# A graph kernel with neighbour sorts: lists found in words of two scores, sorts that leave two columns out, and single-graph sets

## The chip, the cores and the metric

The kernel runs on one core of a Trainium2 chip. The core has five engines with a queue each: TensorE (PE), VectorE (DVE), ScalarE (ACT), GpSimd (POOL) and SyncE (SP). Each works through its instructions in the order in which the program put them, and waits where an operand is not ready. SP issues plain DMAs, POOL the indirect ones. The metric is the device time of one execution in microseconds, the median of several runs; lower is better.

## The reference, cut to what matters

There are 16 graphs of 1024 nodes with 64 features each, and an adjacency matrix for every graph. Layer 0 is a dense message step and a small network. Layer 1 takes, for every node and every feature, three quantiles over the node's neighbours, after a rule has removed up to two of them.

```python
# layer 0
messages = einsum('bij,bjh->bih', adjacency, h)
dh = tanh(concatenate([h, messages], -1) @ W1 + b1) @ W2 + b2
x = layernorm(x + dh)
# layer 1
adj_d = dilate(adj, mask)          # degree m > 10: skip = (m+1)//2, drop every skip-th neighbour
vals = where(valid[..., None], x[:, None, :, :], big)
sv = sort(vals, axis=2)
for tau, wt in zip([0.25, 0.5, 0.75], [0.25, 0.5, 0.25]):
    pos = tau * (m - 1)            # linear interpolation between sv[floor] and sv[ceil]
    agg += wt * q
x = layernorm(x + mlp(x + agg) * mask)
```

The adjacency is sparse and its degree falls with the node number: a few nodes have more than a hundred neighbours, most have under ten.

## The kernel before, in words

The kernel gathers neighbours instead of masking. Its work is written as some twenty generators ("jobs"), which `run_jobs` (L323) interleaves.

**Scheduler.** `Engine` (L234) wraps each engine: it estimates a cost for every instruction and keeps on a `Board` when each engine comes free and when each tile is written. `run_jobs` always takes the step of the job with the smallest `max(ready, engine free) + bias`. A job that moves to another engine gets `HOP` (L214, 1000 ns) added to its ready time. Biases stand in the list at the end of `sparse`: `front` is -300 ns on DVE and -1500 elsewhere, sorts have 0, the ends of units -2000. The resulting order is fixed when the program is built; on the chip each engine follows it.

**Front, per graph.** SP loads adjacency tiles (`a_sb`). DVE makes `score`, a float16 for each neighbour that falls with the column and is 0 elsewhere; SP stores the scores to `score_rows`. PE transposes the tiles and multiplies them into messages, and `layer0` (L617) adds the network and the norm: `pre` and `s_rows` on DVE. The rows go to `score_rows`, to `table`, and for the sets of two graphs to a table of their own, `early`. `places` (L658) ranks nodes by degree.

**Sets.** `SETS` (L194) groups graphs: two pairs and three fours. Within a set, tile `q` takes 128 nodes of like degree, `128 // len(graphs)` from each graph; tile 0 holds the hubs. `LIMITS` bounds the neighbours of a node by its rank. POOL fetches a tile's scores and rows with one indirect DMA (`permuted`, 128x578 words). `listing` (L766) finds the neighbours of its nodes: rounds of `max` (the 8 largest of a row) and `match_replace` (set those to 0). `remove` scatters the removed edges into the tables, so a set's first tiles ("heads") have to be listed before anything is gathered.

**Hubs.** `CLASSES` (L204) collects hub rows of several graphs into tiles of 128: `first_tile` (L856) stores their scores, `hub_lists` (L1064) lists them. The two greatest classes, 1 and 0, are `pair` and the great hub unit; their buffers exist only when the front's memory is free.

**Units.** `UNITS` (L206) groups one to four tiles into a unit, and `plan` orders units and hubs. Per unit:
- `fetch_rows` (L1098) issues one indirect gather on POOL for each neighbour slot of each tile: `X[:, d, k, :]`, 128 rows of 66 words. The last two columns carry what the removals overwrite. `XBUFS` is 4.
- `prepare` compares those two columns with the node's number (`hit`), and ACT adds a very large value (`fill`) to removed neighbours.
- `sort` (L971) runs a merge-exchange network over the slots with `min` and `max` between `X` and `Y`, on DVE.
- `finish` scales the sorted slots with interpolation weights on ACT and sums them on PE (`pa`), runs the network, and POOL scatters the result into `out_dram`.

Nearly all instructions carry the line of the recording helper, so the profile is read by tile names.

Of the kernel before, what the change touches and what calls it, by code (L numbers as in the profile page):

```python
# [11 lines left out]
F32 = mybir.dt.float32  # L12
F16 = mybir.dt.float16
# [10 lines left out]
P = 128  # L24
N = 1024
NT = N // P
C = 64
# [145 lines left out]
def network(n, inner):  # L173
# [5 lines left out]
    for layer in needed_only(merge_exchange(n), need):  # L179
        new = {}  # L180
        for cost, at, ops in beam:
# [9 lines left out]

SETS = ((0, 1), (2, 3), (4, 5, 6, 7), (8, 9, 10, 11), (12, 13, 14, 15))  # L194
ROWS = N + 1
W = C + 2
NX = N // 2 + W
# [3 lines left out]
          (192, 11), (256, 10), (288, 9), (352, 8), (448, 7), (544, 6), (672, 5), (800, 4),  # L201
          (896, 3), (992, 2))

CLASSES = ((0, 8, 16), (8, 8, 16), (16, 8, 16), (24, 8, 16), (32, 32, 4))  # L204

UNITS = {2: ((1,), (2, 3), (4, 5, 6, 7), (8, 9, 10, 11), (12, 13, 14, 15)),  # L206
         4: ((1,), (2,), (3, 4), (5, 6, 7)) + tuple(tuple(range(q, q + 4)) for q in range(8, 32, 4))}
HEADS = 256
PIECE = 1056
# [1 line left out]
AHEAD = 6  # L211
LISTS = 2
XBUFS = 4
HOP = 1000  # L214
LANDS = 1500


def most(slot):

    return min(cap for first, cap in LIMITS if first <= slot)  # L220
# [137 lines left out]
def sparse(ctx, tc, x, adj, nodemask, w1a, b1a, w2a, b2a, w1b, b1b, w2b, b2b, consts, out,  # L358
# [3 lines left out]
    B = x.shape[0]  # L362
    set_of = {b: i for i, graphs in enumerate(SETS) for b in graphs}
    board = Board()
    V, A, T, GP, SY = (Engine(e, k, board) for e, k in zip(
        (nc.vector, nc.scalar, nc.tensor, nc.gpsimd, nc.sync), "VATGS"))
# [5 lines left out]
    fpool = fronts.enter_context(tc.tile_pool(name="s_front", bufs=1))  # L372
# [64 lines left out]
    with tc.tile_pool(name="s_init", bufs=1) as pool:  # L437
# [16 lines left out]
        for b in range(B):  # L454
            V.tensor_copy(info[:, b, :, 0], node_id)
            V.memset(info[:, b, :, 4], float(b - SETS[set_of[b]][0]))
            V.tensor_copy(counts[:, b, NT:], rev)
# [4 lines left out]
    none = fpool.tile([B, W], F32, name="s_none")  # L462
# [4 lines left out]
    for b in range(4, B):  # L467
# [1 line left out]
    tables = dram_disjoint_views(table, B // 4)  # L469

    early = [dram.tile([len(graphs) * ROWS, W], F32, name=f"early{graphs[0]}")
             for graphs in SETS if len(graphs) == 2]
    for t in early:
        SY.dma_start(t.rearrange("(b n) w -> b n w", n=ROWS)[:, N, :], none[0:2, :])
    hub_scores = [dram.tile([B * n, NX], F32, name=f"hub_scores{c}")
                  for c, (_, n, _) in enumerate(CLASSES)]
    hub_infos = [dram.tile([B * n, HI], F32, name=f"hub_infos{c}")
                 for c, (_, n, _) in enumerate(CLASSES)]
    score_rows = [dram.tile([len(graphs) * N, NX], F32, name=f"score_rows{graphs[0]}")
                  for graphs in SETS]  # L480
    own_rows = [dram.tile([len(graphs) * N, W], F32, name=f"own_rows{graphs[0]}")
                for graphs in SETS]
    writes = len(CLASSES) + sum(len(u) for graphs in SETS for u in UNITS[len(graphs)])
    outs = iter(dram_disjoint_views(out, writes))
# [31 lines left out]
    tiles, inputs, turned, scores, nodes, whole = {}, {}, {}, {}, {}, {}  # L516
# [240 lines left out]
    def list_fetches(pool):  # L757
        for n, (i, q) in enumerate(later):
# [4 lines left out]
            permuted(pool, si, q, "permuted", LISTS)  # L763
            yield "G", 0

    def listing(pool, si, qs, kind):  # L766

        K, state = len(qs), sets[si]
        w = P // len(SETS[si])
        caps = [most(q * w) for q in qs]  # L770
        rounds = -(-caps[0] // 8)
        lists = pool.tile([P, K, rounds * 8], F16, tag=f"lists_{kind}", name="lists", bufs=2)
        if -(-caps[-1] // 8) < rounds:
            V.memset(lists[:, :, 8:], 0.0)
        for k, q in enumerate(qs):
            yield "S", lambda q=q: (si, q) in whole
            ps = whole[si, q]
            yield "S", ps
            SY.dma_start(own_rows[si][q * P:(q + 1) * P, :], ps[:, N // 2:])
            yield "V", ps  # L780
            scores = ps[:, :N // 2].bitcast(F16)
            for r in range(-(-caps[k] // 8)):
                if r:
                    V.match_replace(scores, lists[:, k, r * 8 - 8:r * 8], scores, 0.0)
                V.max(lists[:, k, r * 8:r * 8 + 8], scores)
            done[kind] += 1
        sl = slice(qs[0], qs[-1] + 1)
        inf = state["inf"]
        return lists, dict(
            ids=inf[:, sl, 0], degree=inf[:, sl, 2], mask=inf[:, sl, 1],  # L790
            own_rows=[own_rows[si][q * P:(q + 1) * P, :] for q in qs], caps=caps,
            own=state["own"][:, sl] if kind == "headed" else None,
            out_index=[state["out_ids"][:, q:q + 1] for q in qs])
# [12 lines left out]
    def late_lists(pool):  # L806
        for i, (si, c, qs) in enumerate(plan):
            if c is None and qs[0] * P // len(SETS[si]) >= HEADS:
                yield "S", lambda si=si: done["heads"] > si
                lists, u = yield from listing(pool, si, qs, "listed")  # L810
                u["index"] = indices(pool, si, qs, lists)
                units[i] = u
# [158 lines left out]
    def sort(u):  # L971

        X = u["X"]
        _, D, K, _ = X.shape
        inner = K * W
        bufs = u["bufs"] = [X, u["Y"]]

        def wires(i, a0, n1, s1, n2, s2):
            t = bufs[i]
            dims = [t.ap[0]]  # L980
            if n1 > 1:
                dims.append([s1 * inner, n1])
            if n2 > 1:
                dims.append([s2 * inner, n2])
            return bass.AP(tensor=t.tensor, offset=t.offset + a0 * inner,
                           ap=dims + [[1, inner]])

        for kind, sa, sb, d, so, (a0, n1, s1, n2, s2) in network(D, inner)[0]:
            to = 0 if kind == "min" else d
            many = max(1, PIECE // (n2 * inner))  # L990
            for i in range(0, n1, many):
                a, n = a0 + i * s1, min(many, n1 - i)
                V.tensor_tensor(wires(so, a + to, n, s1, n2, s2), wires(sa, a, n, s1, n2, s2),
                                wires(sb, a + d, n, s1, n2, s2),
                                op=ALU.min if kind == "min" else ALU.max)
                yield "V", 0
# [137 lines left out]
    plan = []  # L1134
    for si, graphs in enumerate(SETS):
        for qs in UNITS[len(graphs)]:
            plan.append((si, None, qs))
            if si == len(SETS) - 1 and qs[-1] == 4:
                plan += [(si, 3, (0,)), (si, 2, (0,))]
        if si == 1:  # L1140
            plan.append((si, 4, (0,)))
    hubs = [i for i, p in enumerate(plan) if p[1] is not None]
    heads = [(si, q) for si, graphs in enumerate(SETS) for q in range(1, HEADS * len(graphs) // P)]
    later = [(i, q) for i, (si, c, qs) in enumerate(plan) for q in qs
# [13 lines left out]
    def fetches(pool):  # L1158
        for i, (si, c, what) in enumerate(plan):
            yield "G", lambda i=i, si=si: i in units and done["heads"] > si  # L1160
            if i >= XBUFS:
                yield "G", lambda i=i: done["free"] > i - XBUFS
            u = units[i]
            u["X"] = pool.tile([P, u["caps"][0] + 1, len(what), W], F32, tag="X", name="X",
                               bufs=XBUFS)
            src = table
            if c is None:
                src = early[si] if si < len(early) else tables[SETS[si][0] // 4]
            elif c == 4:
                src = tables[0]  # L1170
            yield from fetch_rows(u, src)
            done["fetch"] += 1
# [66 lines left out]
    with tc.manual_schedule(engines={getattr(mybir.EngineType, e) for e in  # L1239
                                     ("DVE", "Activation", "PE", "Pool", "SP")}):  # L1240
        pool = ctx.enter_context(tc.tile_pool(name="s_body", bufs=2, side="right"))

        def all_fronts_out():
            yield from front_outs(fpool)
            yield "V", lambda: done["rows"] == B
            fronts.close()
            late["pool"] = ctx.enter_context(tc.tile_pool(name="s_hubs", bufs=1))

        def front(engine):
            return -300 if engine == "V" else -1500  # L1250

        def great_bias(engine):
            return 1000 if late.get("sorting") == 0 else -500

        run_jobs(board, [
            Job(ends(pool), -2000),
            Job(preparations(pool), -1000),
            Job(loads(fpool), 0),
            Job(score_tiles(fpool), front),
            Job(sign_tiles(fpool), front),  # L1260
            Job(store_tiles(), front),
            Job(places(fpool), front),
            Job(turn_tiles(fpool), front),
            Job(head_fetches(fpool), front),
            Job(list_fetches(pool), -300),
            Job(late_lists(pool), -300),
            Job(message_tiles(fpool), front),
            Job(layer0(fpool), front),
            Job(all_fronts_out(), front),
            Job(hub_units(pool), -500),  # L1270
            Job(fetches(pool), 0),
            Job(sorts(pool), 0),
            Job(great_fetches(), -700),
            Job(great_units(), great_bias),
        ])
# [512 lines left out]
```

## Time and profile before

| | |
|---|---|
| timed, median of 3 | 3262.88 us (3250.48 to 3291.58) |
| profiled execution | 2980.74 us |
| its span, first to last instruction | 2979.0 us |
| ACT busy, instructions | 1275.4 us, 3836 |
| mean granted PE clock | 0.619 |
| HBM read and written | 159.25 MB, 56.43 MB |
| first and last store of layer-0 rows | 131.8 and 1164.9 us |
| first `permuted` fetch on POOL | 191.7 us |
| first gather of `pair` | 1326.3 us |

The profiled execution and the timed runs differ by 282 us. The views give durations within the profiled one.

The groups of instructions that weigh most (engine, operation, tiles, count, then busy us and mean ns, then idle time before them and what ended it):

```profile
L308 POOL DMA_INDIRECT X<-table,index x756 | 869.9, 1151 | 245.4 <-issue 218.2
L308 POOL DMA_INDIRECT X<-table,hub_ix x256 | 312.4, 1220 | 79.4 <-issue 74.4
L308 DVE TENSOR_TENSOR Y<-X 128x528 f32<-128x528 f32 (+11 forms) x440 | 270.8, 637 | 7.0 <-PE pa L308 3.7
L308 DVE SCALAR_TENSOR_TENSOR score<-a_sb,s_desc 128x1024 f16<-128x1024 f32 x128 | 155.1, 1219 | 104.3 <-DMA a_sb<-in_adj_dram 60.6
```

"issue" is time in which the engine waited for nothing that the profile shows.

### The profile page before, as it was taken

The numbers are of one execution on the slowest core, as the hardware profiler recorded it, in microseconds if no ns is written. First come the engines' busy times: TensorE is split into PE (matmuls) and PEld (weight loads), VectorE is DVE, ScalarE is ACT, GpSimd is POOL, SyncE is SP. The second block draws the span as 40 slices with busy tenths as digits, with TensorE's granted clock in tenths as the row PEclk, the third lists the DMA queues.
The fourth block names the chain that finished last, engine by engine and source line by source line (L and its number), as shares of the span: only waits on it lengthen the run. The fifth ranks groups of instructions, "written<-read, shape, count | busy, mean of one in ns | idle before, by whom it ended". The sixth has DMA issues, their size and how long they took to land.

```text
span 2979.0 us, 23139 instructions
## 1 busy us (share of the span) xinstructions
PE 1264.5 (42%) x5017; PEld 792.8 (27%) x5017; DVE 2148.9 (72%) x4918; ACT 1275.4 (43%) x3836; POOL 1883.6 (63%) x1609
## 2 busy tenths in 40 slices
PE   3767675758566773110413023222234131133337
PEld 2444343434343442110212001221112121111116
DVE  3337678867788876999991058878888887876782
ACT  3666575657666753120511353133243132224423
POOL 0003675265647665667687778778877778888762
PEclk9788776768767775555655555555555555555555
DMA  9555765245525532211101121221111221111100
GB/s 197 139 144 147 189 186 133 81 120 154 133 83 151 144 76 62 51 41 27 24 14 27 27 50 42 45 52 33 24 26 32 49 58 39 39 25 23 25 4 4
DMA packets 202175, 217.37 MB, mean 73 GB/s; under 512 B 136636, under 2 KB 136828, under 8 KB 202028
## 3 DMA queue, kind: packets, MB, share of 16 engines
q1 hardware_dynamic: 132140, 126.23, 15.3%
q0 software_dynamic: 57408, 86.35, 13.2%
q10 hardware_dynamic: 12480, 3.24, 1.0%
q8 instruction: 42, 0.69, 0.1%
q14 instruction: 105, 0.86, 0.1%
HBM read 159.25 MB, written 56.43 MB: 72 GB/s over the span
## 4 chain that ended last, share of the span: by engine, by line
POOL 28%; DVE 15%; issue 9%; DMA 6%; PE 3%; ACT 1%; SPq 0%; POOLq 0%; DVEq 0%; ACTq 0%
POOL X L308 24%; DVE Y L308 3%; DVE X L308 3%; DMA X<-table,index 3%; POOL out_dram L308 3%; PE pa L308 2%; DVE hub_list L308 2%; DVE hub_sc L308 1%; DVE lists L308 1%; DMA permuted<-score_rows,ids 1%; DVE pair L308 1%; POOL permuted L308 1%; DVE permuted L308 1%; DMA X<-table,hub_ix 0%; DVE pre L308 0%
## 5 line engine op out<-in xcount | busy, mean ns | idle before, releaser
L308 POOL DMA_INDIRECT X<-table,index x756 | 869.9, 1151 | 245.4 <-issue 218.2
L308 ACT ACTIVATE X<-X,fill 128x64 f32<-128x64 f32 x1248 | 315.3, 335 | 579.7 <-DVE fill L308 555.1
L308 PE MATMUL pa<-X,s_half_ident 128*128 128x64 f32 (+3 forms) x614 | 204.5, 490 | 480.0 <-ACT X L308 417.9
L308 PE MATMUL pa<-Y,s_half_ident 128*128 128x64 f32 (+3 forms) x568 | 185.3, 467 | 515.7 <-ACT Y L308 483.6
L308 POOL DMA_INDIRECT X<-table,hub_ix x256 | 312.4, 1220 | 79.4 <-issue 74.4
L308 POOL DMA_INDIRECT permuted<-score_rows,ids x128 | 138.4, 1081 | 336.3 <-DMA score_rows<-s_rows 201.0
L308 POOL DMA_INDIRECT X<-early,index x236 | 252.1, 1068 | 129.9 <-issue 68.0
L308 PEld LDWEIGHTS pa<-X,s_half_ident 128*128 128x128 f32 x614 | 141.7, 314 | 538.0 <-ACT X L308 535.5
L308 PE MATMUL pn<-aT,x_sb 128*64 128x256 f32 x1024 | 280.3, 423 | 0.0
L308 PEld LDWEIGHTS pa<-Y,s_half_ident 128*128 128x128 f32 x568 | 127.1, 296 | 572.3 <-ACT Y L308 564.3
L308 POOL DMA_INDIRECT out_dram<-y,out_ids x123 | 200.6, 1631 | 119.9 <-DVE y L308 73.3
L308 DVE TENSOR_TENSOR Y<-X 128x528 f32<-128x528 f32 (+11 forms) x440 | 270.8, 637 | 7.0 <-PE pa L308 3.7
L308 DVE MAX8 lists<-permuted 128x8 f16<-128x1024 f16 x174 | 211.2, 1222 | 35.9 <-DMA permuted<-score_rows,ids 33.6
L308 DVE SCALAR_TENSOR_TENSOR score<-a_sb,s_desc 128x1024 f16<-128x1024 f32 x128 | 155.1, 1219 | 104.3 <-DMA a_sb<-in_adj_dram 60.6
L308 DVE TENSOR_TENSOR X<-Y 128x528 f32<-128x528 f32 (+12 forms) x362 | 226.7, 642 | 2.4
L308 ACT ACTIVATE Y<-Y,wt 128x64 f32<-128x64 f32 x572 | 152.3, 335 | 150.6 <-DVE Y L308 150.6
L308 ACT ACTIVATE X<-X,wt 128x64 f32<-128x64 f32 x610 | 159.4, 334 | 131.6 <-DVE X L308 131.6
L308 PE MATMUL pt<-s_ident,a_sb 128*128 128x128 f32 x1024 | 159.3, 306 | 97.5 <-ACT aT L308 85.1
L308 ACT ACTIVATE junk<-score 128x1024 bf16<-128x1024 f16 x128 | 135.1, 1055 | 113.4 <-DVE score L308 108.6
L308 PEld LDWEIGHTS pn<-aT,x_sb 128*64 128x64 f32 x1024 | 143.9, 151 | 102.0 <-issue 49.8
L308 ACT COPY aT<-pt 128x512 f32<-128x512 f32 x256 | 137.8, 584 | 71.5 <-PE pt L308 71.1
L308 PEld LDWEIGHTS pt<-s_ident,a_sb 128*128 128x128 f32 x1024 | 128.5, 157 | 140.3 <-ACT aT L308 97.5
(168 smaller groups left out, 2804.1 us busy)
## 6 DMA issues: line engine op xcount, KB each, us to landing
a_sb<-in_adj_dram SPq DMA_DIRECT2D x128, 512.0 KB
score_rows<-score SPq DMA_DIRECT2D x128, 256.0 KB
X<-table,index POOLq DMA_INDIRECT x756
score_rows<-s_rows SPq DMA_DIRECT2D x16, 264.0 KB
table<-s_rows SPq DMA_DIRECT2D x16, 264.0 KB
x_sb<-in_x_dram SPq DMA_DIRECT2D x16, 256.0 KB
X<-table,hub_ix POOLq DMA_INDIRECT x256
own_rows<-permuted SPq DMA_DIRECT2D x123, 33.0 KB
```

The source lines that it names most:

```text
L308: return op(*args, **kw)
```

## The change

It has six parts.

1. `SETS` begins with two single-graph sets, so there are six sets instead of five, three of them with an `early` table. `UNITS` gets an entry for them: three units of 1, 2 and 4 tiles per graph.
2. `CLASSES` gets a sixth entry: ranks 64 to 127 of graphs 0 and 1, which lie in tile 0 of the new sets, make one more hub unit of 128 rows.
3. `HOP` is 1500 ns.
4. `listing` reads the 1024 float16 scores as 512 float32 words of two neighbouring scores, takes the `8n` largest words into `pairs`, then the `8n` largest float16 values of those. A word's order is set by its upper half; every word that is not zero is among those taken, since a row has at most `8n` neighbours.
5. The operands of a sort step cover 64 of each tile's 66 columns.
6. `late_lists` gets bias 0 instead of -300; `layer0` gets -1500 on all engines instead of `front`.

```diff
-SETS = ((0, 1), (2, 3), (4, 5, 6, 7), (8, 9, 10, 11), (12, 13, 14, 15))
+SETS = ((0,), (1,), (2, 3), (4, 5, 6, 7), (8, 9, 10, 11), (12, 13, 14, 15))
...
-CLASSES = ((0, 8, 16), (8, 8, 16), (16, 8, 16), (24, 8, 16), (32, 32, 4))
-
-UNITS = {2: ((1,), (2, 3), (4, 5, 6, 7), (8, 9, 10, 11), (12, 13, 14, 15)),
+CLASSES = ((0, 8, 16), (8, 8, 16), (16, 8, 16), (24, 8, 16), (32, 32, 4), (64, 64, 2))
+
+UNITS = {1: ((1,), (2, 3), (4, 5, 6, 7)),
+         2: ((1,), (2, 3), (4, 5, 6, 7), (8, 9, 10, 11), (12, 13, 14, 15)),
...
-HOP = 1000
+HOP = 1500
...
     early = [dram.tile([len(graphs) * ROWS, W], F32, name=f"early{graphs[0]}")
-             for graphs in SETS if len(graphs) == 2]
+             for graphs in SETS if len(graphs) < 4]
     for t in early:
-        SY.dma_start(t.rearrange("(b n) w -> b n w", n=ROWS)[:, N, :], none[0:2, :])
+        SY.dma_start(t.rearrange("(b n) w -> b n w", n=ROWS)[:, N, :], none[0:t.shape[0] // ROWS, :])
...
+    def largest(out, values, n):
+        for r in range(n):
+            if r:
+                V.match_replace(values, out[:, r * 8 - 8:r * 8], values, 0.0)
+            V.max(out[:, r * 8:r * 8 + 8], values)
...
-            scores = ps[:, :N // 2].bitcast(F16)
-            for r in range(-(-caps[k] // 8)):
-                if r:
-                    V.match_replace(scores, lists[:, k, r * 8 - 8:r * 8], scores, 0.0)
-                V.max(lists[:, k, r * 8:r * 8 + 8], scores)
+            n = -(-caps[k] // 8)
+            top = pool.tile([P, 32], F32, tag="pairs", name="pairs")
+            largest(top, ps[:, :N // 2], n)
+            largest(lists[:, k], top[:, :n * 8].bitcast(F16), n)
...
-            return bass.AP(tensor=t.tensor, offset=t.offset + a0 * inner,
-                           ap=dims + [[1, inner]])
+            if K > 1:
+                dims.append([W, K])
+            return bass.AP(tensor=t.tensor, offset=t.offset + a0 * inner, ap=dims + [[1, C]])
...
-        if si == 1:
-            plan.append((si, 4, (0,)))
+        if si in (1, 2):
+            plan.append((si, 6 - si, (0,)))
...
-            elif c == 4:
+            elif c > 3:
                 src = tables[0]
...
-            Job(late_lists(pool), -300),
+            Job(late_lists(pool), 0),
             Job(message_tiles(fpool), front),
-            Job(layer0(fpool), front),
+            Job(layer0(fpool), -1500),
```

## The prediction

> **What bounds the kernel now.** The page's first two parts say which engine is full and when. The three rows below are the busy totals and the 40 slices (74.5 us each) of VectorE and GpSimd.
>
> ```profile
> PE 1264.5 (42%) x5017; PEld 792.8 (27%) x5017; DVE 2148.9 (72%) x4918; ACT 1275.4 (43%) x3836; POOL 1883.6 (63%) x1609
> ...
> DVE  3337678867788876999991058878888887876782
> POOL 0003675265647665667687778778877778888762
> ```
>
> POOL does nothing for two and a half slices. VectorE is thin for the first three slices, full from 1300 us, empty in slice 22. So no average will do, and the second view is busy time by stage (window, then busy us and instructions of PE, weight load, DVE, ACT, POOL, then clock and DMA):
>
> ```profile
> 420.00:1165.00 745.00, 501.31 (x2191) 299.35 (x2189) 594.01 (x1400) 474.78 (x1189) 428.27 (x391) 0.73 0.45 119
> 1165.00:1326.00 161.00, 26.33 (x96) 21.87 (x96) 132.45 (x370) 30.42 (x124) 101.49 (x102) 0.50 0.25 53
> ...
> 1600.00:2826.00 1226.00, 313.87 (x878) 192.39 (x878) 877.67 (x1935) 400.20 (x1588) 967.36 (x827) 0.52 0.17 37
> 2826.00:2979.00 153.00, 79.76 (x315) 66.17 (x315) 87.82 (x228) 48.28 (x187) 65.97 (x13) 0.53 0.01 4
> ```
>
> Three stages follow. **The front**, to 1165 us, when the last graph's layer-0 rows are written: DVE is 80% busy (594 of 745), nothing else above 67%. **The gathers**: from 1326 us, when POOL issues the first gather of the great hub unit (`pair`), to the last at 2824 us. POOL is 79% busy (967 of 1226), and its timeline shows 0.30 us ahead of every instruction; 827 x 0.30 = 248, and 967 + 248 = 1215 of 1226. POOL is the bound. **The tail**, 153 us: the chain of waits ends so (start, length, what):
>
> ```profile
> 2823.80 16.86 issue
> 2840.89 1.21 POOL out_dram L308
> ...
> 2914.99 1.65 DVE X L308 x3
> 2916.64 2.27 DVE Y L308 x5
> 2919.96 47.63 PE pa L308 x222
> ```
>
> The last gather is done at 2824, its unit is prepared at 2826, but DVE sorts the great unit until 2920, and 47.6 us of scaling and summing come after that.
>
> A last view, POOL's timeline around one late gather:
>
> ```profile
> 2696.37 1.75 POOL L308 DMA_INDIRECT X<-table,index  x1 [0.30 <-issue]
> 2698.43 12.18 POOL L308 DMA_INDIRECT X<-table,index  x1 [0.30 <-issue]
> 2710.91 0.94 POOL L308 DMA_INDIRECT X<-table,index  x1 [0.30 <-issue]
> ```
>
> A gather takes 0.94 us in 1600-1700, where DVE is idle; this one took 12.18 beside an unbroken run of DVE sort steps, another 22.62. Behind 1326 us POOL's instructions take 1240 us; at 0.95 each its 1007 would take 957. DVE costs POOL 283 us.
>
> **What the skill says.** "SBUF — State Buffer", section "Who interferes with whom": a DVE instruction with two SBUF inputs contends with a GpSimd instruction that reads SBUF, one with a single input does not. The 12.18 us agree: sort steps have two inputs. "VectorE: DVE Perf Modes", errata section: fp32 `tensor_tensor` takes (N+151)/0.96 ns. The trace agrees: 704 ns at 528 columns (formula 707), 1252 at 1056 (1257). "Perfetto Trace Analysis", "Optimization Strategy": regimes with different busiest engines gain by interleaving. That fits an idle POOL at the start.
>
> **The change, part by part.** Counts are from the order in which the two programs stand on each queue.
>
> *Lists.*
>
> ```profile
> L308 DVE MAX8 lists<-permuted 128x8 f16<-128x1024 f16 x174 | 211.2, 1222 | 35.9 <-DMA permuted<-score_rows,ids 33.6
> ...
> L308 DVE MATCH_REPLACE8 permuted<-lists,permuted 128x1024 f16<-128x1024 f16 x51 | 61.6, 1208 | 0.0
> ```
>
> Gone: 211 + 62 = 273 us. New: 171 maxima and 49 replacements over 512 words, then as many over 16 to 64 halves. No row shows a 512-word maximum; with 1.04 ns an element (from the 704 and 1252 above) it is 1222 - 532 = 690 ns, and 676 for the replacement: 118 + 33 us. The small ones are 150 + 30 ns or so: 40 us. Sum 191, gain 82. If a 4-byte word costs two halves the new lists come to 309 and lose 36. I take 82, since `tensor_tensor` in fp32 already moves one word per cycle.
>
> *Sorts of 64 columns.* Their row elements fall from 916,542 to 892,352 (25 us at 1.04 ns), their instructions rise from 2234 to 2299, 65 at 0.15 = 10 us, because three units become six plus a hub. Net gain 15. The operands get another dimension with a 2-word gap after every 64 columns. Nearest row: the 128x512 write into `s_rows`, 64 of every 66 columns, 693 ns, against 693 for the contiguous `pre<-pre,ln_mean`. So I take 0; a cost of one cycle a run would be 13,900 x 1.04 = 15 us. A gap can't pay, so nothing lies below 0.
>
> *Single-graph sets.* POOL has 8 more instructions (236 to 224 early gathers, 256 to 276 from hubs), 8 x 1.45 = 12 us, in the front where POOL has room. DVE gets one more first tile (scan 2.29, two picks 1.28, one compare 0.42), 5 hub-list passes at 1.22 and some 70 small operations at 0.2: 25 us. ACT gets 41 operations and 8 table loads at 1.28, some 25 us at 43% busy; SP 6 DMAs at 0.4 us. These hide: ACT's and SP's slack in the front; if it is gone they are 28 us. DVE in sum: 82 + 15 - 25 = 72 us less.
>
> *Where that lies.* The bias and HOP edits issue nothing; they only move instructions, so I summed DVE durations by the program's order (fixed part plus elements, as above; the sum exceeds busy time by 9%, as neighbours overlap). Up to the last graph's `s_rows` write: 865 before, 858 after. Behind the last graph but before the last unit's `hit`: unchanged within 10. After that `hit`: 104 before, 50 after. So the order after spends the freed time on earlier sorting, and the surplus is taken out of the tail.
>
> *Front.* Graph 0's rows are stored at 131.8 us, graph 1's at 186.5. POOL's first fetch, at 191.7, needs graph 1 now; it will need graph 0: 55 us earlier. The first X gather follows by more, since it stands 12 POOL instructions in instead of 18. Sorting moves into the thin slices: to graph 5 the order has 276 us of DVE work instead of 233, from there to graph 15 582 instead of 632. Intervals between stores fit max(55, 1.13 x DVE work between): that gives 1006 us before (measured 1033) and 965 after. **Gain 41.** Bounds: 0 if loads or PE pace the front; 80 if its waits shrink too. Layer 0 ahead of sorts and the 1500 ns hop move `pre` past sort steps; queued behind it are those sorts only, and POOL has 600 of its instructions in 1130 us to cover it.
>
> *New waits.* The first unit's `hit` now stands on DVE between the two halves of graph 2's `pre`; queued behind it are that half, `place` and graph 3's scores, and PE and ACT wait for those. Its 14 gathers stand behind 20 POOL instructions from 137 us; with head lists near 187 us they land near 220, and graph 2's `pre` came at 228. Cost 0, at worst the 30 us that the early gathers could be late. The new hub's gathers read `table` and stand on POOL behind the last removals of graphs 2 and 3, which wait for DVE's lists as they did; the longest such wait was 19 us.
>
> *Gathers.* POOL has 1007 instructions from `pair` on, before and after. **Gain 0**: a faster DVE waits for POOL there, as slice 22 shows. So starting POOL early is worth only what `pair` moves.
>
> *Tail.* DVE ends 94 us behind the last `hit`. After, the great sort's last step stands behind the last unit's `y`, which comes 48 us after that `hit` (2873.7). So 94 becomes 48, and the 47.6 us of summing remain. **Gain 46.**
>
> Sum 87 of the profiled 2979 (2980.7 with what lies around it): 2892. The timed runs have a median of 3262.9, 282 more than that execution; no view shows where. Taking 87 off gives 3176, scaling by 0.971 gives 3168. I take **3170**.
>
> **Rivals.**
> - *Only the tail pays.* In the front PE is at 67% and its clock falls to 0.5 later; if timed runs start throttled, PE paces the front and DVE's relief is hidden. 3263 - 46 = 3217, or 3263 if the surplus great sort starves POOL as well. For it: the unexplained 282 us. Against: DVE's 80%.
> - *More than forecast.* Units free their buffers earlier, POOL's gaps before 1326 (315 us beyond the 0.30) shrink by half, and the front drops 80 with 100 less starvation: near 3040.
> - *Slower: gathers starve.* Sort steps with four-dimensional operands hold the shared read port longer, or run unbroken more often, and each POOL gather waits. The price is today's 283 us from 1326 on. It decides from 283 + 152 (87 gained, 65 for 2%), half as much again. At twice the price: 3263 - 87 + 283 = 3460; at 1.6 times 3345. For it: the 12 us gather. Against: 24,000 fewer elements to sort.
> - *It does not do what it says*: maxima of words cost double. 82 + 36 = 118 us of DVE come back, mostly in the front: near 3270.
>
> **Numbers.** Forecast 0.53, only the tail 0.21, words cost double 0.06, more than forecast 0.07, starvation 0.13. Faster by over 2% (below 3198; 2% is about what a measurement can tell) takes the forecast and the better case: 0.60. Within 2%, the tail and the double cost: 0.27. Slower, starvation: 0.13. The range leaves out most of the starvation case and the far end of the better one: 3075 to 3275.
>
> **What would show it.** First POOL fetch near 137 us; last `s_rows` store near 1125; `pair` near 1285; still about 1500 us from `pair` to the last gather; DVE's end within 50 us of the last `hit`; 512-word maxima at 0.69 us; 512-column sort steps at 0.69. It is wrong if the time from `pair` to the last gather changes by over 60 us, if the last store stays at 1165, or if the sort rows rise.

## The result, and the profile after

| | before | after |
|---|---|---|
| timed, median of 20 | 3261.35 us | 3234.14 us (3187.76 to 3265.33) |
| ratio | | 0.9883, interval 0.985 to 0.9917 |
| profiled execution | 2980.74 us | 3236.20 us |

The change makes the kernel 27 us faster, where 93 were forecast (3262.9 to 3170). The kernel before takes about 2990 us in some comparisons and 3260 to 3285 us in others, each made on one chip; the profile of before that the prediction used was of the first kind, and the times of both kernels and the profile of after are of the second. Below, "the 2990 group" and "the 3260 group" are the comparisons in which the kernel before took the one or the other.

The page of after, busy totals and the 40 slices (80.9 us each) of VectorE and GpSimd:

```profile
PE 1327.3 (41%) x5075; PEld 822.5 (25%) x5075; DVE 2071.0 (64%) x5327; ACT 1300.6 (40%) x3877; POOL 1794.4 (55%) x1617
...
DVE  3446666664768576679793005768988757748782
POOL 0025363454323475665487673867787757866751
```

VectorE has 78 us less work (2148.9 to 2071.0; forecast 72), and POOL starts a slice earlier. But both are emptier than before through most of the front and of the gathers. By stage (front from the first store of layer-0 rows to the last, `pair` to the last gather, tail; window, then busy us and instructions of PE, weight load, DVE, ACT, POOL, then clock and DMA):

```profile
130.00:1312.00 1182.00, 744.74 (x3191) 439.94 (x3188) 738.12 (x2077) 668.11 (x1569) 526.24 (x502) 0.72 0.45 115
...
1484.00:3126.00 1642.00, 410.92 (x1118) 253.08 (x1118) 1105.95 (x2552) 475.30 (x1839) 1145.81 (x994) 0.51 0.15 31
3126.00:3234.00 108.00, 77.82 (x311) 65.32 (x311) 43.35 (x119) 47.47 (x186) 15.46 (x14) 0.55 0.02 5
```

In the front VectorE is busy 738 of 1182 us, 62%; in the profile of before it was 762 of 1033, 74%, between the same two stores. From `pair` to the last gather POOL has 994 instructions of 1146 us and 0.30 us ahead of each: 1146 + 298 = 1444 of 1642, so it waits 198 us for something else, where the profile of before had 26. The tail is 108 us instead of 153. The chain's end shows why (start, length, what):

```profile
3172.52 50.62 PE pa L309 x236
```

VectorE's last sort step ends at 3174, 45 us behind the last `hit` (3129), and only the great unit's summing is left. The prediction had worked out 48 us. The new list instructions in the table of groups:

```profile
L309 DVE MAX8 pairs<-permuted 128x8 f32<-128x512 f32 x171 | 117.9, 689 | 28.9 <-DMA permuted<-score_rows,ids 25.4 <-DVE permuted L309 1.3 <-issue 0.3
L309 DVE MATCH_REPLACE8 permuted<-pairs,permuted 128x512 f32<-128x512 f32 x49 | 33.1, 676 | 0.0
L309 DVE MAX8 lists<-pairs 128x8 f16<-128x16 f16 (+3 forms) x171 | 32.5, 190 | 39.6 <-remote 24.7 <-issue 6.3 <-DVE pairs L309 3.2
L309 DVE MATCH_REPLACE8 pairs<-lists,pairs 128x32 f16<-128x32 f16 (+2 forms) x49 | 9.0, 184 | 0.0
```

Their sum is 192.5 us; the forecast said 191. But the small maxima have 39.6 us of idle time ahead of them, of which 31.0 end with "remote" (a queue that the profile doesn't know) or "issue". So the new instructions cost what they should, and the time went elsewhere.

### The profile page after: what moved, and what is told of

Its sections match the earlier page's. It is cut to its first block, busy times and chain, and to the rows that moved or that the text cites. A ratio compares the mean times of both kernels' runs of the same rounds, so it can differ in the third digit from the quotient of the medians.

```text
span 3234.3 us, 23763 instructions
## 1 busy us (share of the span) xinstructions
PE 1327.3 (41%) x5075; PEld 822.5 (25%) x5075; DVE 2071.0 (64%) x5327; ACT 1300.6 (40%) x3877; POOL 1794.4 (55%) x1617
## 4 chain that ended last, share of the span: by engine, by line
DVE 24%; POOL 23%; issue 15%; PE 14%; ACT 10%; another core or an unknown queue 7%; DMA 4%; DVEq 0%; POOLq 0%; SPq 0%; ACTq 0%
POOL X L309 20%; DVE Y L309 5%; ACT junk L309 4%; DVE X L309 4%; PE pn L309 4%; PE pa L309 3%; POOL out_dram L309 3%; PE pt L309 2%; ACT X L309 2%; DVE pairs L309 2%; DVE hub_list L309 2%; PE pd L309 2%; PE rows L309 1%; DVE hub_sc L309 1%
## 5 line engine op out<-in xcount | busy, mean ns | idle before, releaser
L309 POOL DMA_INDIRECT X<-table,index x756 | 842.9, 1115 | 252.7 <-issue 225.0
L309 ACT ACTIVATE X<-X,fill 128x64 f32<-128x64 f32 x1256 | 326.8, 336 | 424.9 <-DVE fill L309 324.1
L309 PE MATMUL pa<-Y,s_half_ident 128*128 128x64 f32 (+3 forms) x578 | 193.7, 478 | 553.3 <-ACT Y L309 356.7
L309 POOL DMA_INDIRECT out_dram<-y,out_ids x122 | 163.3, 1339 | 270.7 <-DVE y L309 101.7
L309 POOL DMA_INDIRECT X<-early,index x224 | 231.2, 1032 | 96.3 <-issue 64.7
L309 DVE TENSOR_TENSOR Y<-X 128x128 f32<-128x128 f32 (+11 forms) x460 | 267.8, 605 | 19.3 <-remote 11.0
L309 PE MATMUL pt<-s_ident,a_sb 128*128 128x128 f32 x1024 | 165.8, 314 | 183.9 <-ACT aT L309 156.3
L309 DVE TENSOR_TENSOR X<-Y 128x512 f32<-128x512 f32 (+14 forms) x378 | 225.2, 611 | 14.2 <-remote 8.4
L309 ACT ACTIVATE junk<-keys,nkey 128x1024 bf16<-128x1024 f32 x128 | 142.3, 1112 | 27.1 <-issue 11.1
```

The costliest lines, as they stand in the source:

```text
L309: return op(*args, **kw)
```

## The experiments

### The same two programs in both groups

The kernel before, unchanged, in two comparisons:

> The kernel before, unchanged, profiled once more. Stall theory: the profiled execution of 2981 us was not like the timed ones (3236 to 3292); this one takes 3240 to 3290, its instructions are as long as before, and the 280 us more are idle time on every engine with no named cause (issue, unknown queue), part of it ahead of POOL's gathers. Rival, cost-moving theory: the profile is near 2981 again and without such idle time, so that the kernel after has to be explained against it, and its 250 us more are its own doing. Time ratio 1.000 in both.

> The kernel before once more, beside the kernel after. What is wanted is the pair of both kernels under one condition, since so far the kernel before was profiled only where it takes 2980 to 3004, and the kernel after only where the kernel before takes 3260 to 3285. If the execution takes about 3280: VectorE's idle time that ends with no named cause (issue, unknown queue, its own last result) is 300 to 450 us, as in the four kernels profiled there, against 34 to 65 where it takes 3000; POOL's waiting beyond 0.30 us an instruction is about 450 in the front and 200 from the first gather of the pair to the last gather, against 297 and 24. If it takes about 2990: 34 to 65, 297 and 24 again.

The kernel after, unchanged, in three:

> The kernel after, unchanged, beside the kernel before and beside the runs that undo one part. If the kernel before takes about 2990 here: the theory that the ratio belongs to the two programs gives 0.988, 2955; the theory that the earlier comparison was made where both programs had some 250 us of idle time that is not theirs, and that the change pays mostly for that time, gives another ratio: 2955 to 3060, and the sum of the parts tried so far (0 + 61 + 71) would give 3123 without the scheduler's part. If the kernel before takes about 3260 here: 3234 again.

> The kernel after once more, beside the kernel before. If the kernel before takes about 2990 here: POOL's waiting in the front, 297 us in the kernel before, is 400 to 420 as in the runs with the sets alone and the columns alone, and the time is 3000 to 3060, slower than before by up to 2%; by the forecast's own sum it would be 2900. If the kernel before takes about 3280: 3270 again.

> The kernel after once more, for the two above. Where the kernel before takes about 3260: 3215 to 3275 again. Where it takes about 2990: POOL's waiting in the front 400 us or so against 297, the tail 104 against 153, in sum 2990 to 3060.

Measured, with the kernel before beside each:

| run | before | this | ratio |
|---|---|---|---|
| e0, before | 2992.4 | 2991.3 | 0.999 (0.9974 to 1.0006) |
| e8, before | 3261.9 | 3261.3 | 1.0004 (0.9971 to 1.0037) |
| e14, after | 2990.1 | 2892.4 | 0.9694 (0.9653 to 0.9735) |
| e9, after | 3261.9 | 3216.7 | 0.988 (0.9801 to 0.9958) |
| e4, after | 3284.5 | 3275.4 | 0.9969 (0.994 to 0.9998) |

The expectation of 3000 to 3060 for e14 was wrong: there the change is worth 98 us. In the other group it is worth 9 to 45. e0 came out near 2991, so the idle time that the stall theory expected was not in it; e8 and e9 had to show it. Busy time by stage (from the first store of rows to the last, to `pair`, to the last gather, to the end) shows where they part. The 2990 group, before (e0):

```profile
134.00:1182.00 1048.00, 713.12 (x3142) 423.88 (x3140) 763.20 (x1766) 655.63 (x1529) 538.04 (x494) 0.75 0.51 129
1182.00:1344.00 162.00, 26.36 (x96) 21.90 (x96) 132.48 (x370) 30.43 (x124) 102.59 (x102) 0.50 0.27 52
1344.00:2846.00 1502.00, 389.91 (x1116) 244.98 (x1116) 1120.79 (x2420) 471.61 (x1872) 1178.80 (x994) 0.52 0.18 34
2846.00:3001.00 155.00, 81.28 (x315) 66.66 (x315) 87.84 (x228) 48.27 (x187) 59.56 (x13) 0.52 0.01 4
```

After (e14):

```profile
130.00:1143.00 1013.00, 713.33 (x3192) 427.13 (x3190) 738.14 (x2077) 666.42 (x1569) 536.95 (x497) 0.76 0.55 134
1143.00:1306.00 163.00, 25.40 (x96) 21.58 (x96) 136.40 (x440) 38.71 (x158) 108.35 (x107) 0.50 0.28 54
1306.00:2786.00 1480.00, 389.96 (x1118) 244.44 (x1118) 1103.87 (x2553) 464.21 (x1839) 1169.15 (x994) 0.52 0.18 35
2786.00:2893.00 107.00, 77.57 (x311) 65.27 (x311) 42.90 (x116) 47.45 (x186) 15.11 (x13) 0.55 0.02 5
```

The 3260 group, before (e8):

```profile
132.00:1288.00 1156.00, 735.74 (x3133) 431.27 (x3131) 762.59 (x1766) 655.82 (x1529) 529.26 (x494) 0.73 0.47 117
1288.00:1464.00 176.00, 26.07 (x96) 21.81 (x96) 132.59 (x370) 30.52 (x124) 100.57 (x102) 0.50 0.25 48
1464.00:3076.00 1612.00, 401.31 (x1116) 249.64 (x1116) 1121.41 (x2416) 483.39 (x1872) 1161.12 (x994) 0.51 0.16 32
3076.00:3234.00 158.00, 84.46 (x315) 68.16 (x315) 88.97 (x233) 48.28 (x187) 66.08 (x14) 0.50 0.01 4
```

After (e9):

```profile
130.00:1297.00 1167.00, 751.81 (x3194) 442.77 (x3192) 736.91 (x2074) 668.81 (x1569) 528.16 (x497) 0.71 0.48 116
1297.00:1480.00 183.00, 25.40 (x96) 21.59 (x96) 137.27 (x443) 40.17 (x158) 111.02 (x108) 0.50 0.25 49
1480.00:3102.00 1622.00, 405.35 (x1118) 251.33 (x1118) 1106.39 (x2551) 474.57 (x1839) 1145.19 (x994) 0.51 0.16 32
3102.00:3210.00 108.00, 79.19 (x311) 66.31 (x311) 43.50 (x119) 47.47 (x186) 15.60 (x14) 0.53 0.02 5
```

Read down a column: DVE's busy time in each stage is the same in both groups (763.20 and 762.59; 738.14 and 736.91), only the windows are longer. Read the windows:

| effect of the change, us | forecast | e0 to e14 | e8 to e9 |
|---|---|---|---|
| start of `pair` | -41 | -39 | +15 |
| `pair` to the last gather | 0 | -21 | +11 |
| tail | -46 | -48 | -50 |
| sum | -87 | -108 | -24 |

These are single executions: by the medians the change is worth 98 and 45 us where the two sums say 108 and 24. The tail pays in both. The front and the gathers pay only in the 2990 group. There VectorE is idle 1048 - 763 = 285 us of the front before and 275 after; in the 3260 group 393 before and 430 after. What this idle time is, ScalarE's timeline shows best. One unit gets its `fill` in 125 operations. In e14 (start, length, operation, count, idle time before and what ended it):

```profile
1649.01 23.96 ACT L309 ACTIVATE X<-X,fill 128x64 f32<-128x64 f32 x100 [93.13 <-DVE fill L309]
...
1681.82 6.07 ACT L309 ACTIVATE X<-X,fill 128x64 f32<-128x64 f32 x25 [8.56 <-DVE fill L309]
```

The same stretch in e9:

```profile
1854.90 20.36 ACT L309 ACTIVATE X<-X,fill 128x64 f32<-128x64 f32 x85
...
1895.12 0.35 ACT L309 ACTIVATE X<-X,fill 128x64 f32<-128x64 f32 x1 [1.05 <-issue]
1896.52 0.35 ACT L309 ACTIVATE X<-X,fill 128x64 f32<-128x64 f32 x1 [1.05 <-issue]
1897.23 0.35 ACT L309 ACTIVATE X<-X,fill 128x64 f32<-128x64 f32 x1 [0.35 <-issue]
```

In e14 an operation starts each 0.24 us (23.96 / 100). In e9 85 of them do so; then most start 0.70 or 1.40 us apart, each 0.35 us long, and for nearly all the profile names nothing that they wait for. VectorE has such stretches too, and TensorE has 410 us of such idle time in e9 and none in e14; POOL's 0.30 us don't change. Summed over VectorE's timeline, idle time that ends with "issue", an unknown queue or VectorE's own last result is 32 us in e0 and 35 in e14, but 224 in e8 and 349 in e9; ScalarE's is 1 in both, but 462 and 456. (For e8, 300 to 450 us on VectorE were expected.) On the chain that ended last, "issue" and the unknown queue make 9% of the span in e0 and 13% in e14, but 13% in e8 and 22% in e9.

From e8 to e9 the change takes 81 us of work from VectorE and adds 125 us of this idle time: work and such idle together go from 2183 to 2104 us in the 2990 group, from 2376 to 2420 in the other. Most of the 125 lie between `pair` and the last gather (92 us in e8, 206 in e9). In the front there is as much in both, 105 and 104 us, so VectorE's own stretches aren't what takes the front's gain away. What grew there is idle time that ends with another engine or a DMA: 262 to 295 us, against 256 to 239 from e0 to e14. The greatest rise is in the wait of layer 0's `pre` for TensorE's result `pd`, 14 us in e8 and 84 in e9, against 26 and 58. TensorE and ScalarE have idle stretches in the front themselves; that these make `pd` late is likely, but no run separates it.

The stretches are not noise. Set instruction by instruction against e14, VectorE waits over 0.8 us longer at 134 places in the profile of after, at 142 in e4 and at 131 in e9; any two of them share 73 to 85 places, where chance would give 3 or 4.

### One part alone

The lists alone:

```diff
-            scores = ps[:, :N // 2].bitcast(F16)
...
+            largest(top, ps[:, :N // 2], n)
+            largest(lists[:, k], top[:, :n * 8].bitcast(F16), n)
```

> Only the lists from words; sets, sort columns and scheduler constants as before. DVE work falls by 82 us in both theories. Give-and-take theory (each part keeps its effect, some other part loses what this one wins): 45 to 80 us faster, 3180 to 3215. Stall theory (in the timed executions VectorE does not pace the front, so less work on it shows only in part): 0 to 25 us faster, 3235 to 3260; its 440 instructions more on VectorE cost as much as they save if instructions themselves are what is short.

The sort columns alone:

```diff
-            return bass.AP(tensor=t.tensor, offset=t.offset + a0 * inner,
-                           ap=dims + [[1, inner]])
+            if K > 1:
+                dims.append([W, K])
+            return bass.AP(tensor=t.tensor, offset=t.offset + a0 * inner, ap=dims + [[1, C]])
```

> Only the sort steps on 64 of 66 columns. 25 us less of DVE work in the steps if a gap costs nothing; mean of a 512-column step 0.69 us against 0.70 at 528. Give-and-take theory: 10 to 25 us faster, as the steps lie beside the gathers and in the tail. Stall theory: 0 to 10 us faster. If gaps hurt (rows of 512 columns at 0.72 us or more, gathers beside sorts longer than 1.15 us in the mean): slower by 10 to 50 us.

The single-graph sets with their hub class and units alone:

```diff
-SETS = ((0, 1), (2, 3), (4, 5, 6, 7), (8, 9, 10, 11), (12, 13, 14, 15))
+SETS = ((0,), (1,), (2, 3), (4, 5, 6, 7), (8, 9, 10, 11), (12, 13, 14, 15))
...
```

> Only the two single-graph sets with the sixth hub class; lists, sort columns and scheduler constants as before. POOL's first fetch moves from 192 to about 137 us in both. Give-and-take theory: the earlier start is worth 10 to 40 us, less 25 us of added DVE and 12 us of added POOL work: between 30 us faster and 15 us slower, 3230 to 3275. Stall theory: the added instructions cost more than they weigh, 15 to 50 us slower, 3275 to 3310.

The scheduler's constants alone:

```diff
-HOP = 1000
+HOP = 1500
...
-            Job(late_lists(pool), -300),
+            Job(late_lists(pool), 0),
...
-            Job(layer0(fpool), front),
+            Job(layer0(fpool), -1500),
```

> Only the scheduler's constants changed. If layer 0 in front of the sorts is what shortens the front: last store of layer-0 rows 20 to 60 us earlier than in the kernel before, the gathers' stage as much longer or shorter as the lists and sorts put off make it: 0 to 50 us faster. If the constants only repair what the other parts spoil: within 15 us of before. If each reordering of a tuned order loses: 20 to 80 us slower.

Measured: lists 0.9997 (0.9983 to 1.0012), columns 1.0194 (1.0168 to 1.022), sets 1.0232 (1.0208 to 1.0257), all beside 2992.4; constants 1.025 (1.0187 to 1.0312) beside 3284.5. No part alone is a gain, though VectorE's work moves as forecast: 2150.9 in e0, 2075.8 with the lists (-75), 2122.9 with the columns (-28), 2170.8 with the sets (+20). The losses of the columns (61 us) and of the sets (71) lie outside all that was expected of them.

With the lists alone the tail falls from 155 to 106 us and `pair` comes 42 us earlier, but only because POOL's order has 68 instructions fewer ahead of `pair` and 68 more from it to the last gather (1062 against 994), and that stretch takes 93 us longer. With the columns alone the front is the loss; its window in e2:

```profile
133.00:1278.00 1145.00, 706.13 (x3144) 416.18 (x3142) 762.71 (x1778) 655.49 (x1543) 535.06 (x511) 0.73 0.49 120
```

VectorE's work in it is that of e0 (762.71 against 763.20), and the window is 97 us longer. The shorter sort steps cost nothing themselves: 512 columns take 0.69 us, the (N+151)/0.96 ns of the Trainium skill's "VectorE: DVE Perf Modes" although the operand leaves out 2 of 66 columns. What changed is the order that the scheduler makes of the new costs: from the 418th on, VectorE's instructions stand in another order than in e0.

The profiles name one price of such orders. In the front VectorE waits for the fetch of a list's rows (what waits and for what, us in total, times, longest), first e0, then e2:

```profile
DVE lists L308 <- DMA permuted<-score_rows,ids: 17.9, 10, 5.0
...
DVE lists L308 <- DMA permuted<-score_rows,ids: 91.3, 14, 36.4
```

The same wait is 89 us with the lists alone and 79 with the sets alone. With all three parts but the old constants (e6, below) it is 87; with the new constants it is 29 in e14, 22 in e9 and 19 in e4. So with the old constants any one of the other parts left VectorE standing at lists whose rows had not come, and the three constants together take most of that away. Which of the three does it was not tried.

Alone, the constants store the last rows at 1251 us (1288 in e8, of another comparison of the group), but POOL has 107 instructions more from `pair` to the last gather (1101), and that stretch takes 219 us longer than in e8.

### One part undone

Each edit is one of the four above, taken back in the kernel after. Without the sets (so with lists, columns and constants), three times:

> The kernel after with the first two graphs as one set again (five sets, five hub classes). The sets alone cost 71 us (87 of them ahead of the last store of layer-0 rows). If that cost is theirs: 40 to 70 us faster than the kernel after. If it came only from the old biases, with which layer 0 stood behind the earlier units' sorts: within 20 us of the kernel after, or slower by up to 40, as POOL's first fetch moves back from 137 to about 195 us.

> The kernel after with the first two graphs as one set, once more. If the kernel before takes about 2990 here: 40 to 70 us faster than the kernel after, so 2940 to 3000. If the kernel before takes about 3280: 30 us faster than the kernel after, 0.989 of before, again.

> The kernel after with the first two graphs as one set. Where the kernel before takes about 3260: 30 to 40 us faster than the kernel after, as twice before. Where it takes about 2990: 40 to 70 us faster than the kernel after.

Without the constants, without the lists, without the columns:

> The kernel after with the scheduler's constants as before (hop 1000 ns, late lists -300, layer 0 with the front's bias). If lists, columns and sets simply add: 130 us above the kernel before. If the constants are what keeps the front short: last store of layer-0 rows 60 to 100 us later than in the kernel after, and 50 to 130 us slower than it. If they do nothing: within 20 us of the kernel after.

> The kernel after with the lists from 1024 scores as before: 266 VectorE instructions fewer, 82 us more of VectorE work. If the work counts: 30 to 80 us slower than the kernel after. If the number of instructions counts where idle time without a cause appears: equal to the kernel after within 15 us there, or faster. If neither counts, because POOL's instructions and its waits set the time: within 20 us of the kernel after in both conditions.

> The kernel after with sort steps over all 66 columns. By the forecast's sum (25 us of sort elements): 5 to 25 us slower than the kernel after. If the columns' price is what it was alone (61 us slower, by the order that it made): up to 60 us faster. POOL's gathers, 1.12 us in the mean, at 1.15 to 1.17.

| undone | before | kernel after | this | ratio to before |
|---|---|---|---|---|
| sets (e15) | 2990.1 | 2892.4 | 2856.1 | 0.9544 (0.9516 to 0.9573) |
| sets (e10) | 3261.9 | 3216.7 | 3178.9 | 0.9766 (0.9673 to 0.9858) |
| sets (e5) | 3284.5 | 3275.4 | 3246.0 | 0.9891 (0.9841 to 0.9941) |
| columns (e13) | 2990.1 | 2892.4 | 2971.2 | 0.9932 (0.9913 to 0.995) |
| lists (e11) | 3261.9 | 3216.7 | 3319.9 | 1.0197 (1.012 to 1.0274) |
| constants (e6) | 3284.5 | 3275.4 | 3367.8 | 1.0252 (1.0192 to 1.0313) |

Lists, columns and constants are each worth 79 to 103 us inside the whole, and nothing or less alone: they don't add. For lists and columns this is more than the work they take away (82 and 25 us by the forecast) and more than was expected of e11 and e13 (at most 80 and 25 us slower). Part of it is order again: from `pair` to the last gather POOL has 1062 instructions in e11 and 1025 in e13, against 994 in the kernel after. e6 keeps the 994; its last rows are stored 31 us later than in e4, where 60 to 100 were expected, the gathers take 51 us longer and the tail 27. e11 had 269 VectorE instructions fewer and 75 us more of its work than e9; it was 103 us slower, so the number of instructions alone doesn't set the time in the 3260 group either. The sets cost 29 to 38 us in both groups. Their price lies in the front. Without them (e15):

```profile
131.00:1100.00 969.00, 698.69 (x3141) 415.85 (x3139) 712.32 (x1929) 653.72 (x1531) 516.79 (x479) 0.78 0.56 139
```

against 1013 us with 738.14 of DVE in e14. POOL's first fetch comes 59 us earlier with the sets, but the last rows are stored 43 us later, and `pair` starts 41 us later. The version without sets beats both kernels in every comparison.

### Holding the first units back

The early unit of graph 0 was suspected: it stands on VectorE ahead of graph 3's layer 0, whose store is 18 us later in e14 than without sets, and 45 us later in e9 than in e10.

```diff
+            if i == 0:
+                yield "G", lambda: done["rows"] >= 4
             if i >= XBUFS:
```

> The kernel after, with the first unit's gathers held back until graph 3's layer-0 rows are written in the program's order, so that no unit's work stands ahead of it on VectorE. If that order is what the sets cost: the store of graph 3 comes at about 300 us instead of 344, the last store at about 1250 instead of 1297, and the time falls by 25 to 45 us against the kernel after. If the cost is the added work itself (25 us on VectorE, 12 on POOL, 25 on ACT): graph 3's store earlier, the last store within 15 us of the kernel after, the time within 15 us.

Measured: 2986.6 us beside 2892.4 for the kernel after, 94 us slower. The expectation fails. Graph 3's store comes 9 us earlier than in e14, as it should, but the front as a whole is longer:

```profile
132.00:1208.00 1076.00, 713.66 (x3161) 424.83 (x3158) 717.87 (x1986) 650.59 (x1517) 511.87 (x472) 0.74 0.49 124
```

VectorE has 20 us less to do there than in e14, and is idle 358 us instead of 275, of which it waits 158 instead of 101 for DMAs. The edit moved more than the one unit: 31 of POOL's instructions went from ahead of `pair` to behind it (1025 against 994). So it doesn't isolate the suspected order, and what makes the sets cost their 29 to 38 us stays open. With them 26 us more of VectorE's work lie in the front (738 against 712), and the front is 44 us longer (1013 against 969); that the added work is the price is not shown.

### Moving the instructions

To learn whether the slow stretches belong to a place in an engine's stream, VectorE and ScalarE got 64 one-column writes more at the start:

```diff
+    for k in range(64):
+        nc.vector.memset(pads[:, 0:1], 0.0)
+        nc.scalar.copy(pads[:, 1:2], ident[:, 0:1])
```

> The kernel after with 64 one-column writes more on VectorE and on ScalarE at the very start, where both wait for the first loads; every later instruction stands 64 places further back in its engine's stream, the order is unchanged. Where the kernel before takes about 2990: 0.969 of it within 10 us, as the 128 instructions are covered. Where it takes about 3260: if the stretches of slow starts belong to a position in the stream, they come at other work than in the kernel after (the stretch at the great hub's list, at 1545 us, goes or moves by about 64 instructions), and the time may move by up to 40 us either way; if they belong to the work, they stay at the hub's list and the time is within 15 us of the kernel after (0.988 to 0.997 of before).

> As for the same kernel before. Where the kernel before takes about 2990: 0.966 again. Where it takes about 3260: if the stretches of slow starts belong to a position in the stream, the one at the great hub's list (about 1545 us) goes or moves by about 64 instructions, and the time may move by up to 40 us either way; if they belong to the work, it stays at the hub's list and the time is 0.988 to 0.997 of before.

Both fell in the 2990 group: 0.9656 (0.962 to 0.9693) and 0.9704 (0.9647 to 0.9761), as the kernel after. They show that the 128 instructions are free there; the question itself was not answered.

## Why the prediction was wrong

**The step that failed** is "Taking 87 off gives 3176, scaling by 0.971 gives 3168. I take **3170**". The 87 were worked out on the profiled execution, and for executions like it the sum is near: where before takes 2990, after takes 98 less. The step carried them over to executions 282 us longer, of which the prediction itself said "no view shows where". The later profiles show where most of such time lies: e8 is 232 us longer than e0, with the same instructions in the same order and as much work on VectorE (2152 and 2151 us), and idle time without a named cause is 192 us more on VectorE and 461 on ScalarE. In those executions the term "Gain 41" of the front measured 15 us of loss (start of `pair`, e8 to e9), and the gathers' 0 measured 11 of loss; with the tail's 50 that is 24 of 87. By the medians it is 45, so of the tail's 50 the front and the gathers together gave back between 5 and 26. Why the front gains nothing there stays open; the wait for `pd` is where it shows.

Point by point:
- First fetch at 137 us: 135.5. 512-word maxima and 512-column steps 0.69 us: 0.689 and 0.69. Lists, 191 us: 192.5. Columns, 25 us of sort elements: 28. Sets, 25 us of VectorE: 20. VectorE in sum 72 less: 78 in the profile of after.
- Tail, gain 46: 48 and 50. "DVE's end within 50 us of the last `hit`" holds for the great unit's sorting (45 us). The 2873.7 given for the last unit's `y` is where POOL stores it; VectorE writes it at 2871.5, also 45 us behind the `hit`.
- Gathers, gain 0, wrong beyond 60: -21 and +11. POOL's gathers became a little shorter (1159 to 1137 ns in the mean, e0 to e14), not longer.
- Front: last store 1182 to 1143 in the 2990 group, 39 us against the 41; 1288 to 1297 in the other. Even where the number is met, its reason is not: without the sets, whose early start was to help the front, the last rows are stored at 1100 (e15), and the sets take 43 of those 82 us back. That the balance came to 39 is luck. And with VectorE's work taken from the traces, "Intervals between stores fit max(55, 1.13 x DVE work between)" gives 1036 us for e0 (measured 1048) and 1073 for e2 (measured 1145). Over the front VectorE's idle time ranges from 257 to 382 us in the 2990 group, with the order. That the order after was a good one, the sum of work didn't tell.
- The single-graph sets were to gain by POOL's earlier start, and their added work to hide. In sum they cost 29 to 38 us in every comparison, though POOL does start 59 us earlier (e15 to e14).
- Layer 0 ahead of the sorts was put at no cost, as "queued behind it are those sorts only". But `pre` itself now waits longer for `pd` in the front, 58 us instead of 26 (e0 to e14) and 84 instead of 14 (e8 to e9).

Of the rivals, "only the tail pays" came near in its number: 3217 forecast, 3216.7 in e9 and 3234 in the first comparison, though 3275 in e4. Its reason, PE pacing the front, is not what the profile shows: PE is busy 752 of 1167 us in e9's front, 64%, and has idle time without a named cause as the others do. Starved gathers and words at double cost are refuted by POOL's 1137 ns and the 689 ns.

## What to carry to other kernels

If a profiled execution is far from the timed median, a sum made on it holds for executions like it only, and the case in which stages full of idle time don't shrink deserves a large chance. Where a scheduler makes the order from costs, the effect of a part is that of the new order, so try parts by undoing them in the whole: alone they may show nothing or the opposite. Work taken from the busiest engine shortens a stage only if that engine's idle time in it stays, so watch the idle time and not the busy share.

## What the runs showed of the hardware

The same program took 9% longer in one comparison than in another (2991 us in e0, 3261 in e8), with as much work on VectorE and POOL's 0.30 us unchanged. Four chips gave about 2990 us and two 3260 to 3285; each was used in one comparison, so whether this belongs to the chip or to the hour is not shown. In the added time VectorE and ScalarE start instructions in steps of 0.7 us: of VectorE's 131 to 142 late starts, 42 to 50 come 1.4 us after the start before, and 13 to 17 come 0.7 us after it. Many fall on the same instructions in different executions. The Trainium skill's "Runtime: NRT & Kernel Launch", section "Instruction fetch mechanics", says that engines stream their instructions in blocks and that this is mostly hidden. The records don't show it as the cause: e14 and e9 have the same 166 packets of the instruction queues, with means of 1159 and 1130 ns on the one and 390 and 407 ns on the other queue. Whether an engine waited for one of them isn't shown. What causes the stretches was not settled.
